# Layers 2 and 3 of a graph network: row buffers for slots, products over their input, expert sums on GpSimd, a last layernorm in two operations

## The chip, the core and the metric

The kernel runs on one core of one Trainium2 chip. The metric is the device time of one execution in microseconds: the time before is the median of five runs. The engines go by the profile's names: PE is TensorE (PEld its weight loads), DVE VectorE, ACT ScalarE, POOL GpSimd, SP SyncE, which here only issues DMAs (its queue is SPq). All data are 32-bit floats.

## The reference

`x` has 1875 nodes of 256 values. Four layers follow, each a graph block and a feed-forward block, both added to `x` after a layernorm. The change is in the last two layers:

```python
# layer 2, graph: two normalized graph convolutions
h = relu(gcn_conv(layernorm(x), edges, weight, W1, b1)); h = gcn_conv(h, edges, weight, W2, b2)
x = x + softmax(h)
# layer 2, feed-forward: 8 experts, the best two by softmax(xt @ Wr + br); xt = layernorm(x)
xn = layernorm(xt) * ln_g[e] + ln_b[e]
x = x + sum over the two experts e of weight_e * (gelu(xn @ W1[e] + b1[e]) @ W2[e] + b2[e])
# layer 3, graph; xl = layernorm(x)
x = x + xl + relu(gcn_conv(xl, edges, weight, W, b))
# layer 3, feed-forward: 16 experts, the best two by xt @ gate_w + gate_b; xt = layernorm(x)
y = xt + sum over the two experts e of weight_e * (relu(xt @ w1[e] + b1[e]) @ w2[e] + b2[e])
x = x + layernorm(y) * gamma + beta
```

`gcn_conv` scales by the inverse root of the degrees on both sides of an adjacency matrix with edge weights.

## The kernel before

The 1875 nodes are padded to 15 tiles of 128 (`NT` = 15, the last one with 83 true rows), and `self.x` holds them all on the chip as `[128, 15, 256]`. The weighted adjacency matrix was built in layer 0 as 15 dense column tiles in DRAM. The code is written for a framework that puts every instruction on its engine in an order that it plans itself, and inserts the waits; tiles come from pools, and the room of a closed pool is given to the next one, which waits for what used it. A tile in a pool with `bufs=n` has n buffers in turn.

**A graph convolution** is `fast_gcn`. Its first loop turns each tile on PE (`turned`, L495, copied from PSUM by ACT as `xT`, L496), multiplies with the weight (`ph`, L1017) and scales into `h` (L1019). Its second loop makes each output tile as 15 products `adj[t][:, u] x h[:, u]` in PSUM (`acc`, L1023), adds (`o`, L1026), scales and adds the bias (`v`, L1028), and calls `done`. In layer 2 it runs twice, as `d0` and `d1`, both with an `h` of their own; in layer 3 once, as `d2`, with `h` written over the input (`inplace`). The adjacency tiles are loaded by `adjacency_tiles` (L995).

**Routing** runs behind the last convolution of a layer: `route_behind` calls `route2` or `route3` for groups of tiles `RG` (four of 3 tiles, one of 2, one of 1), one group after the tile that follows it, the last two after the last tile. A route makes a layernorm (`rxl` in layer 2, `f3y` in layer 3), the router's logits, the two best experts, and a slot for each (node, expert) by counts over the nodes before. Then it fills `rows`, `[128, g, 2, 258]`: the 256 values twice, a gate (L1753) and the token's number (L1754), and sends them to DRAM by indirect DMAs from POOL, one for each tile and choice, six for a group of three (`scatter`, L1122). `rows` lies in a pool with one buffer. In layer 2 the fill is a second layernorm on DVE (L1194) and a copy on ACT (L1929), in layer 3 two copies on ACT (L1961).

**The experts** (`few_experts`) take tiles of 256 slots, load each tile's expert weights, and scatter weighted outputs to `r.outs`. After the last scatter has landed (`done`, L1139) the two rows of each node are summed: for each of 15 tiles one DMA on SP loads both into `s` (L1892, six buffers), and DVE adds the one and then the other into `acc` (L1894), which is `self.x` in layer 2 and `r.y` (`f3y`) in layer 3.

**The end** (`layer3_ffn`): in chunks of 3 tiles the layernorm of `f3y` into `z` (L1194), times gamma (L1205), plus beta (L1206), plus `self.x` (L1977), and a store (L1979, and L1981 for the last 83 rows).

`layernorm` makes statistics for each tile (L1187, L1188), then a chain of small operations for the inverse root (L1190, a Sqrt on ACT at L1167, L1174 to L1179), then one operation for each tile. In the graph blocks of layers 2 and 3 it goes in groups of 5 tiles; in layer 3 POOL then adds it to `x` in three operations (L1073).

Of the kernel before, what the change touches and what calls it, by code (L numbers as in the profile page):

```python
# [31 lines left out]
F32 = mybir.dt.float32  # L32
I32 = mybir.dt.int32
BF16 = mybir.dt.bfloat16
AF = mybir.ActivationFunctionType
# [5 lines left out]
P = 128  # L41
# [33 lines left out]

SL = 256
SH = SL // P

RG = [range(0, 3), range(3, 6), range(6, 9), range(9, 12), range(12, 14), range(14, 15)]

# [17 lines left out]
class Net:  # L98
# [900 lines left out]
    def gcn_weights(self, sb, i, w, b):  # L999
        return self.weight(sb, w, f"gw{i}"), self.vector_row(sb, b, f"gb{i}")  # L1000

    def fast_gcn(self, pre, x, adj, wb, done, inplace=False):


        nc, tc = self.nc, self.tc
        with ExitStack() as ctx:
            one = ctx.enter_context(tc.tile_pool(name=f"{pre}6", bufs=1))
            sb = ctx.enter_context(tc.tile_pool(name=f"{pre}7", bufs=2))
            ps = ctx.enter_context(tc.tile_pool(name=f"{pre}9", bufs=2, space=PSUM))
            w, b = wb  # L1010
            h = x if inplace else one.tile([P, NT, D], F32, name="h")
            for t in range(NT):
                xT = sb.tile([P, KD, P], F32, name="xT")
                self.turned(xT, x[:, t, :], ps)
                p = ps.tile([P, D], F32, name="ph")
                for kc in range(KD):
                    nc.tensor.matmul(p, xT[:, kc, :], w[:, kc, :], start=kc == 0,  # L1017
                                     stop=kc == KD - 1)
                nc.vector.tensor_scalar(h[:, t, :], p, self.dinv[:, t:t + 1], None, op0=ALU.mult)  # L1019
            for t in range(NT):  # L1020
                acc = ps.tile([P, D], F32, name="acc")
                for u in range(NT):
                    nc.tensor.matmul(acc, adj[t][:, u, :], h[:, u, :], start=u == 0,  # L1023
                                     stop=u == NT - 1)
                o = sb.tile([P, D], F32, name="o")
                nc.vector.tensor_tensor(o, h[:, t, :], acc, ALU.add)  # L1026
                v = sb.tile([P, D], F32, name="v")
                nc.vector.scalar_tensor_tensor(v, o, self.dinv[:, t:t + 1], b,  # L1028
                                               op0=ALU.mult, op1=ALU.add)
                done(t, v, sb, ps)  # L1030

    def fast_layer2_gnn(self, r):
        nc, tc, a = self.nc, self.tc, self.a
        with tc.tile_pool(name="q2a", bufs=1) as ap, tc.tile_pool(
            name="q2", bufs=1
        ) as one, tc.tile_pool(name="q2r", bufs=1) as rp:
            ws = [self.gcn_weights(one, i, a[f"L2_gnn_W{i}"], a[f"L2_gnn_b{i}"]) for i in (1, 2)]
            adj = self.adjacency_tiles(ap)
            y = one.tile([P, NT, D], F32, name="y")
            with tc.tile_pool(name="q2n", bufs=3) as sb:  # L1040
                self.layernorm_by(y, self.x, sb, 5)

            def relu(t, v, sb, ps):
                nc.scalar.activation(y[:, t, :], v, AF.Relu)

            def softmax(t, v, sb, ps):
                mx = sb.tile([P, 1], F32, name="mx")
                nc.vector.tensor_reduce(mx, v, AX.X, ALU.max)
                nc.vector.tensor_scalar(mx, mx, -1.0, None, op0=ALU.mult)
                e = sb.tile([P, D], F32, name="e")  # L1050
                sm = sb.tile([P, 1], F32, name="sm")
                nc.scalar.activation(e, v, AF.Exp, bias=mx, accum_out=sm)
                nc.vector.reciprocal(sm, sm)
                nc.vector.scalar_tensor_tensor(self.x[:, t, :], e, sm, self.x[:, t, :],
                                               op0=ALU.mult, op1=ALU.add)
                self.route_behind(self.route2, r, t, rp, ps)

            self.fast_gcn("d0", y, adj, ws[0], relu)
            self.fast_gcn("d1", y, adj, ws[1], softmax)

    def fast_layer3_gnn(self, r):
        nc, tc, a = self.nc, self.tc, self.a
        with tc.tile_pool(name="q3a", bufs=1) as ap, tc.tile_pool(
            name="q3", bufs=1
        ) as one, tc.tile_pool(name="q3r", bufs=1) as rp:
            ws = self.gcn_weights(one, 3, a["L3_gnn_W"], a["L3_gnn_b"])
            adj = self.adjacency_tiles(ap)
            xl = one.tile([P, NT, D], F32, name="xl")
            with tc.tile_pool(name="q3n", bufs=3) as sb:
                self.layernorm_by(xl, self.x, sb, 5)  # L1070
                for t in range(0, NT, 5):
                    v = self.x[:, t:t + 5, :]
                    nc.gpsimd.tensor_tensor(v, v, xl[:, t:t + 5, :], ALU.add)  # L1073
# [7 lines left out]
            self.fast_gcn("d2", xl, adj, ws, add, True)  # L1081

# [98 lines left out]
    def layernorm(self, out, x, sb):  # L1181
# [11 lines left out]
        for t in range(n):  # L1193
            nc.vector.tensor_scalar(out[:, t, :], x[:, t, :], mv[:, t, 0:1], rs[:, t:t + 1],  # L1194
                                    op0=ALU.subtract, op1=ALU.mult)

    def layernorm_by(self, out, x, sb, n):

# [474 lines left out]
    def router(self, name, en, w, b, sb):  # L1673
# [24 lines left out]
                       allow_small_or_imprecise_dtypes=True)  # L1698
        return r

    def route(self, r, ts, x, fill, weigh, sb, ps):


# [29 lines left out]
        at = sb.tile(shape, F32, name="at")  # L1733
        nc.vector.tensor_tensor(at, r.seen[:, sl, :], counts[1], ALU.add)
        nc.vector.tensor_tensor(at, at, r.base[:, None, :].to_broadcast(shape), ALU.add)
        rows = sb.tile([P, g, 2, D + 2], F32, name="rows")
        fill(rows)
        for i in range(2):
            pick = sb.tile(shape, F32, name="pick")
# [74 lines left out]
    def few_experts(self, pre, r, act, f, acc, w1n, w2n, b2n, affine):  # L1814
# [7 lines left out]
        with ExitStack() as ctx:  # L1822
# [64 lines left out]
            with tc.tile_pool(name=f"{pre}s", bufs=2) as sb:  # L1887
                for t in range(NT):
                    n = min(P, N - t * P)
                    s = sb.tile([P, 2, D], F32, name="sum", bufs=6)  # L1890
                    v = r.outs[0:2 * NP, :].rearrange("(i n) d -> n i d", i=2)
                    self.behind(nc.sync.dma_start(s[:n], v[t * P:t * P + n]), done)  # L1892
                    for i in range(2):
                        nc.vector.tensor_tensor(acc[:n, t, :], acc[:n, t, :], s[:n, i, :], ALU.add)  # L1894

    def prepare_experts(self, sb):

# [12 lines left out]
    def route2(self, r, ts, sb, ps):  # L1910
        nc = self.nc
        g = len(ts)
        xl = sb.tile([P, g, D], F32, name="rxl")
        self.layernorm(xl, self.x[:, ts[0]:ts[0] + g, :], sb)

        def weigh(lo, sb):
            pr = sb.tile([P, g, R], F32, name="pr")
# [7 lines left out]
            return hots, tops  # L1925

        def fill(rows):
            self.layernorm(rows[:, :, 0, 0:D], xl, sb)
            nc.scalar.copy(rows[:, :, 1, 0:D], rows[:, :, 0, 0:D])  # L1929

        self.route(r, ts, xl, fill, weigh, sb, ps)

# [56 lines left out]
    def route_all(self, route, r):  # L1989
        with self.tc.tile_pool(name="ra", bufs=2) as sb, self.tc.tile_pool(  # L1990
            name="rap", bufs=2, space=PSUM
        ) as ps:
            for ts in RG:
                route(r, ts, sb, ps)

# [248 lines left out]
```

## Time and profile before

| | |
|---|---|
| median of 5 runs | 3758.53 us (3757.52 to 3762.1) |
| the profiled execution's own time | 3758.14 us |
| its span, first to last instruction | 3756.3 us |
| mean granted TensorE clock | 0.887 |
| busy: PE, DVE, ACT, POOL | 2896.1, 1892.9, 924.6, 1548.5 us |
| products of `d0`, solid on PE | 2600.3 to 2695.6 us |
| products of `d1` with routing between them | 2717.0 to 2844.6 |
| rest of layer 2's routing | 2844.6 to 2882.0 |
| layer 2's experts | 2882.0 to 3229.0 |
| sums, layernorm of layer 3 | 3229.0 to 3268.4 |
| first loop of `d2` | 3268.4 to 3290.8 |
| products of `d2` with routing | 3290.8 to 3408.9 |
| rest of layer 3's routing | 3408.9 to 3437.5 |
| layer 3's experts | 3437.5 to 3700.3 |
| sums | 3700.3 to 3723.6 |
| last layernorm and stores | 3723.6 to 3756.3 |

The lower rows were read from the order of time. Busy time is time in which the engine worked on an instruction, and its idle time matters only where the next step waits for it. A line such as "DVE rows L1754 <- DMA f_slots<-rows,slot" means that VectorE was idle before its instruction of line 1754, which writes `rows`, and that the last thing to release it was a DMA that reads `rows` and writes `f_slots`. An "x3" counts instructions that were merged into a line of the timeline.

### The profile page before, as it was taken

To read this page: it belongs to the slowest core of one execution; us is meant where nothing else is said; L and a number is where in the kernel's file an instruction comes from. 1 tells how busy PE (TensorE), PEld (TensorE's weight loads), DVE (VectorE), ACT (ScalarE), POOL (GpSimd) and SP (SyncE) were. 2 spreads that over 40 slices of the span, in tenths; PEclk is the share of its full clock that TensorE was granted. 3 is DMA by queue.
4 is the path that set the end of the run, shared out by engine and by line. 5 is a ranking of instruction groups with operands and counts; after the bars stand their busy time and mean duration, and the time that the engine had idled before them with its cause. 6 is when DMAs were issued, how large, how long until landed. Compare 5 with 4: busy or idle time off the path is not lost. (4 is left out here: it accounts for less than half of the span.)

```text
span 3756.3 us, 43452 instructions
## 1 busy us (share of the span) xinstructions
PE 2896.1 (77%) x14049; PEld 2405.9 (64%) x14049; DVE 1892.9 (50%) x5542; ACT 924.6 (25%) x1998; POOL 1548.5 (41%) x1546
## 2 busy tenths in 40 slices
PE   3878789979997999668745654985995999596993
PEld 2667678858876777446534444654874888475772
DVE  5566576756765776683256663015254111444234
ACT  1333233323332333213211110210132222122221
POOL 2777577747775777100277861001011111112220
PEclk9999899989998999889866765997997999798996
DMA  5434656655664543113444431524003555503663
GB/s 147 124 109 129 200 158 201 181 152 162 186 194 129 141 115 114 41 38 96 150 130 132 138 102 38 163 79 170 1 22 97 188 182 183 212 31 110 205 202 120
DMA packets 330704, 495.34 MB, mean 132 GB/s; under 512 B 79601, under 2 KB 258724, under 8 KB 328676
## 3 DMA queue, kind: packets, MB, share of 16 engines
q1 hardware_dynamic: 254612, 289.88, 24.5%
q0 software_dynamic: 72672, 199.68, 18.0%
q10 hardware_dynamic: 3184, 2.91, 0.2%
q8 instruction: 113, 1.85, 0.2%
q14 instruction: 123, 1.01, 0.1%
HBM read 369.90 MB, written 122.43 MB: 131 GB/s over the span
## 5 line engine op out<-in xcount | busy, mean ns | idle before, releaser
L1116 POOL DMA_INDIRECT g<-qt,w_src x1056 | 1033.7, 979 | 431.3 <-issue 350.5
L621 PE MATMUL acc<-m,s 128*128 128x256 f32 (+1 forms) x2112 | 559.9, 389 | 16.3 <-ACT m L608 16.3
L592 PE MATMUL pe<-ew,w_attr 128*128 128x256 f32 x1888 | 509.4, 395 | 72.3 <-DVE g L607 71.5
L607 DVE TENSOR_TENSOR g<-g,pe 128x512 f32<-128x512 f32 x528 | 360.5, 683 | 394.0 <-DMA g<-qt,w_src 327.2
L608 ACT ACTIVATE m<-g 128x512 f32<-128x512 f32 x528 | 332.6, 631 | 791.1 <-DVE g L607 604.5
L1116 POOL DMA_INDIRECT g<-rq_h,w_tsrc x264 | 305.5, 1157 | 391.1 <-PE pz L886 311.2
L592 PEld LDWEIGHTS pe<-ew,w_attr 128*128 128x128 f32 x1888 | 364.8, 197 | 155.5 <-DVE g L607 95.5
L621 PEld LDWEIGHTS acc<-m,s 128*128 128x128 f32 x2112 | 404.5, 196 | 65.3 <-ACT m L608 17.5
L1874 PE MATMUL hid<-xeT,w 128*128 128x256 f32 x1184 | 272.9, 387 | 23.5 <-DVE xeT L1869 23.5
L1880 PE MATMUL out<-w,hidT 128*128 128x256 f32 x1184 | 264.0, 379 | 0.0
L1874 PEld LDWEIGHTS hid<-xeT,w 128*128 128x128 f32 x1184 | 222.1, 193 | 62.8 <-DVE xeT L1869 30.8
L1876 ACT ACTIVATE hidT<-hid,cols 128x256 f32<-128x256 f32 x296 | 138.2, 474 | 447.3 <-PE hid L1874 447.3
L1880 PEld LDWEIGHTS out<-w,hidT 128*128 128x128 f32 x1184 | 225.1, 190 | 30.5
L1122 POOL DMA_INDIRECT f_slots<-rows,slot x60 | 58.3, 972 | 416.2 <-DVE pick L1740 248.6
L599 DVE TENSOR_TENSOR s<-iota,w_dst 128x256 f32<-128x256 f32 x528 | 219.8, 417 | 0.0
L399 PE MATMUL padj<-col,row 128*128 128x240 f32 x720 | 206.5, 382 | 14.5 <-DVE col L372 13.0
L1023 PE MATMUL acc<-h,adj 128*128 128x256 f32 x900 | 207.4, 389 | 0.0
L1883 DVE TENSOR_TENSOR ye<-out,b 128x256 f32<-128x256 f32 x104 | 44.1, 424 | 313.9 <-PE out L1880 313.9
L1023 PEld LDWEIGHTS acc<-h,adj 128*128 128x128 f32 x900 | 172.7, 195 | 22.4
L1122 POOL DMA_INDIRECT f_outs<-ye,f2place x44 | 42.7, 970 | 302.4 <-DVE ye L1884 276.5
L399 PEld LDWEIGHTS padj<-col,row 128*128 128x128 f32 x720 | 142.1, 199 | 36.3 <-DVE col L372 9.9
L372 DVE TENSOR_SCALAR col<-wide,g_col,g_wt 128x240 f32<-128x240 f32 x360 | 147.3, 409 | 0.0
(416 smaller groups left out, 4070.6 us busy)
## 6 DMA issues: line engine op xcount, KB each, us to landing
f_slots<-zeros SPq DMA_DIRECT2D x45, 1032.0 KB
w<-in_L_ffn_W SPq DMA_DIRECT2D x44, 1024.0 KB
adj<-adj SPq DMA_DIRECT2D x45, 960.0 KB
w<-in_L_ffn_w SPq DMA_DIRECT2D x60, 512.0 KB
w<-in_L_ffn_w SPq DMA_DIRECT2D x18, 1024.0 KB
g<-qt,w_src POOLq DMA_INDIRECT x1056
dstrow<-lin SPq DMA_DIRECT2D x14, 1152.0 KB
rq_h<-hr SPq DMA_DIRECT2D x8, 1980.0 KB
```

The source lines that it names most:

```text
L372: pin(nc.vector.tensor_scalar(col, self.wide, self.gcol[:, i:i + 1], self.gwt[:, i:i + 1], op0=ALU.is_equal, op1=ALU.mult))
L399: pin(nc.tensor.matmul(pa[:, u // GT, :], row, col, start=u % GT == 0, stop=u % GT == GT - 1))
L592: pin(nc.tensor.matmul(pes[q][:, v, :], at[:, v, :], self.ew[:, i, :], start=True, stop=True))
L599: pin(nc.vector.tensor_tensor(ss[q], self.iota[:, None, :].to_broadcast([P, 2, P]), self.wdst[:, c:c + 2, None].to_broadcast([P, 2, P]), A ...
L607: pin(nc.vector.tensor_tensor(g, g, pes.pop(q), ALU.add))
L608: pin(nc.scalar.activation(m[:, :, :D], g, AF.Relu))
L621: pin(nc.tensor.matmul(accs[t], s[:, v, :], m[:, v, :], start=k == v == 0, stop=end and v == 1))
L1023: nc.tensor.matmul(acc, adj[t][:, u, :], h[:, u, :], start=u == 0, stop=u == NT - 1)
L1116: self.nc.gpsimd.indirect_dma_start(out=out, out_offset=None, in_=table, in_offset=bass.IndirectOffsetOnAxis(ap=at, axis=0))
L1874: nc.tensor.matmul(p1, w1[:, kc, m * P:(m + 1) * P], xT[:, kc, :], start=kc == 0, stop=kc == KD - 1)
L1876: nc.scalar.activation(hT[:, m, :], p1, act, bias=v[:, m:m + 1])
L1880: nc.tensor.matmul(p2, hT[:, m, i * P:(i + 1) * P], w2[:, m, :], start=m == 0, stop=m == fc - 1)
```

## The change

`rows` is no longer a tile of its own: `rows_in` cuts two buffers out of a given tile, and each route takes the other one. In layer 2 that tile is `first`, which holds the first convolution's input and, as both convolutions now write over their input, its products; in layer 3 it is a tile `rowbufs`. The layernorms of the graph blocks go in groups of 3, and layer 3's sum with `x` is made on POOL tile by tile. `layernorm` is cut in two, `moments` and the scaling. The fill of layer 2 becomes six ACT operations with a scale and a bias. The sums of the expert outputs have 15 buffers, loads on two queues (SP and ACT), the sum of the two rows on POOL and one add on DVE. At the end beta is added to `x` ahead of the experts on POOL, and the last layernorm is two operations for each tile, in place, without `z`.

```diff
+ROWS = 2 * CH * 2 * (D + 2)
...
-    def fast_gcn(self, pre, x, adj, wb, done, inplace=False):
+    def fast_gcn(self, pre, x, adj, wb, done):
...
-            one = ctx.enter_context(tc.tile_pool(name=f"{pre}6", bufs=1))
...
-            h = x if inplace else one.tile([P, NT, D], F32, name="h")
+            h = x
...
+            first = one.tile([P, NT, D], F32, name="first")
             y = one.tile([P, NT, D], F32, name="y")
+            self.rows_in(r, first)
             with tc.tile_pool(name="q2n", bufs=3) as sb:
-                self.layernorm_by(y, self.x, sb, 5)
+                self.layernorm_by(first, self.x, sb, CH)
...
-            self.fast_gcn("d0", y, adj, ws[0], relu)
+            self.fast_gcn("d0", first, adj, ws[0], relu)
...
+            self.rows_in(r, one.tile([P, 1, ROWS], F32, name="rowbufs"))
             with tc.tile_pool(name="q3n", bufs=3) as sb:
-                self.layernorm_by(xl, self.x, sb, 5)
-                for t in range(0, NT, 5):
-                    v = self.x[:, t:t + 5, :]
-                    nc.gpsimd.tensor_tensor(v, v, xl[:, t:t + 5, :], ALU.add)
+                for t in range(0, NT, CH):
+                    self.layernorm(xl[:, t:t + CH, :], self.x[:, t:t + CH, :], sb)
+                    for u in range(t, t + CH):
+                        nc.gpsimd.tensor_tensor(self.x[:, u, :], self.x[:, u, :], xl[:, u, :],
+                                                ALU.add)
...
+    def rows_in(self, r, buf):
+        flat = buf.rearrange("p t d -> p (t d)")
+        n = ROWS // 2
+        r.rows = [flat[:, i * n:(i + 1) * n].rearrange("p (g i d) -> p g i d", i=2, d=D + 2)
+                  for i in range(2)]
...
-        rows = sb.tile([P, g, 2, D + 2], F32, name="rows")
+        r.rows.append(r.rows.pop(0))
+        rows = r.rows[0][:, :g]
         fill(rows)
...
-                    s = sb.tile([P, 2, D], F32, name="sum", bufs=6)
+                    s = sb.tile([P, 2, D], F32, name="sum", bufs=NT)
                     v = r.outs[0:2 * NP, :].rearrange("(i n) d -> n i d", i=2)
-                    self.behind(nc.sync.dma_start(s[:n], v[t * P:t * P + n]), done)
-                    for i in range(2):
-                        nc.vector.tensor_tensor(acc[:n, t, :], acc[:n, t, :], s[:n, i, :], ALU.add)
+                    queue = nc.scalar if t % 2 else nc.sync
+                    self.behind(queue.dma_start(s[:n], v[t * P:t * P + n]), done)
+                    nc.gpsimd.tensor_tensor(s[:n, 0, :], s[:n, 0, :], s[:n, 1, :], ALU.add)
+                    nc.vector.tensor_tensor(acc[:n, t, :], acc[:n, t, :], s[:n, 0, :], ALU.add)
...
         def fill(rows):
-            self.layernorm(rows[:, :, 0, 0:D], xl, sb)
-            nc.scalar.copy(rows[:, :, 1, 0:D], rows[:, :, 0, 0:D])
+            mv, rs = self.moments(xl, sb)
+            low = sb.tile([P, g], F32, name="rlow")
+            nc.vector.scalar_tensor_tensor(low, mv[:, :, 0], -1.0, rs, op0=ALU.mult, op1=ALU.mult)
+            for i in range(2):
+                for j in range(g):
+                    nc.scalar.activation(rows[:, j, i, 0:D], xl[:, j, :], AF.Identity,
+                                         bias=low[:, j:j + 1], scale=rs[:, j:j + 1])
...
-        self.few_experts("e3", r, AF.Relu, 2 * D, y, "L3_ffn_w1", "L3_ffn_w2", "L3_ffn_b2", False)
         with tc.tile_pool(name="f3b", bufs=1) as one, tc.tile_pool(name="f3s", bufs=3) as sb:
-            z = one.tile([P, NT, D], F32, name="z")
             gam = self.vector_row(one, a["L3_ffn_gamma"], "gam")
             bet = self.vector_row(one, a["L3_ffn_beta"], "bet")
+            for t in range(NT):
+                nc.gpsimd.tensor_tensor(self.x[:, t, :], self.x[:, t, :], bet, ALU.add)
+            self.few_experts("e3", r, AF.Relu, 2 * D, y, "L3_ffn_w1", "L3_ffn_w2", "L3_ffn_b2",
+                             False)
             for t in range(0, NT, CH):
-                v, ts = z[:, t:t + CH, :], slice(t, t + CH)
-                self.layernorm(v, y[:, ts, :], sb)
-                self.affine(v, gam, bet)
-                nc.vector.tensor_tensor(v, v, self.x[:, ts, :], ALU.add)
+                ts = slice(t, t + CH)
+                v = y[:, ts, :]
+                mv, rs = self.moments(v, sb)
+                for j in range(CH):
+                    u = v[:, j, :]
+                    nc.vector.scalar_tensor_tensor(u, u, mv[:, j, 0:1], gam, op0=ALU.subtract,
+                                                   op1=ALU.mult)
+                    nc.vector.scalar_tensor_tensor(u, u, rs[:, j:j + 1], self.x[:, t + j, :],
+                                                   op0=ALU.mult, op1=ALU.add)
```

More of the change, by code (lines that the diff above doesn't have):

```diff
@@ L1079, in add @@
                 self.route_behind(self.route3, r, t, rp, ps)
-            self.fast_gcn("d2", xl, adj, ws, add, True)
+            self.fast_gcn("d2", xl, adj, ws, add)
     def first_edges(self):
@@ L1179, in inverse, with moments @@
         nc.vector.tensor_tensor(out, r, q, ALU.mult)
-    def layernorm(self, out, x, sb):
+    def moments(self, x, sb):
         nc = self.nc
@@ L1192, in layernorm @@
         self.rsqrt(rs, ve, sb)
-        for t in range(n):
-            nc.vector.tensor_scalar(out[:, t, :], x[:, t, :], mv[:, t, 0:1], rs[:, t:t + 1],
-                                    op0=ALU.subtract, op1=ALU.mult)
+        return mv, rs
+    def layernorm(self, out, x, sb):
+        mv, rs = self.moments(x, sb)
+        for t in range(x.shape[1]):
+            self.nc.vector.tensor_scalar(out[:, t, :], x[:, t, :], mv[:, t, 0:1], rs[:, t:t + 1],
+                                         op0=ALU.subtract, op1=ALU.mult)
     def layernorm_by(self, out, x, sb, n):
@@ L1913, in route2 @@
         xl = sb.tile([P, g, D], F32, name="rxl")
-        self.layernorm(xl, self.x[:, ts[0]:ts[0] + g, :], sb)
+        mv, rs = self.moments(self.x[:, ts[0]:ts[0] + g, :], sb)
+        for j in range(g):
+            nc.vector.tensor_scalar(xl[:, j, :], self.x[:, ts[0] + j, :], mv[:, j, 0:1],
+                                    rs[:, j:j + 1], op0=ALU.subtract, op1=ALU.mult)
         def weigh(lo, sb):
@@ L1927, in fill @@
         def fill(rows):
-            self.layernorm(rows[:, :, 0, 0:D], xl, sb)
-            nc.scalar.copy(rows[:, :, 1, 0:D], rows[:, :, 0, 0:D])
+            mv, rs = self.moments(xl, sb)
+            low = sb.tile([P, g], F32, name="rlow")
+            nc.vector.scalar_tensor_tensor(low, mv[:, :, 0], -1.0, rs, op0=ALU.mult, op1=ALU.mult)
+            for i in range(2):
+                for j in range(g):
+                    nc.scalar.activation(rows[:, j, i, 0:D], xl[:, j, :], AF.Identity,
+                                         bias=low[:, j:j + 1], scale=rs[:, j:j + 1])
         self.route(r, ts, xl, fill, weigh, sb, ps)
@@ L1992, in route_all @@
         ) as ps:
+            self.rows_in(r, sb.tile([P, 1, ROWS], F32, name="rowbufs", bufs=1))
             for ts in RG:
```

## The prediction

> **What bounds the kernel now.** I read the chain that ended last, then a table of stretches that I cut at the borders of layers 2 and 3, then the waits inside them, then the order of time around each. The change touches nothing before 2564 us. First the stretches (busy us per engine, granted clock, DMA share, GB/s):
>
> ```profile
> core 0: us, PE busy (x) PEld busy (x) DVE busy (x) ACT busy (x) POOL busy (x), PEclk, DMA share, GB/s
> 2717.00:2844.60 127.60, 114.41 (x524) 99.57 (x522) 72.58 (x365) 41.02 (x76) 20.72 (x21) 0.91 0.06 22
> 2844.60:2882.00 37.40, 6.85 (x26) 5.61 (x26) 21.86 (x149) 9.74 (x17) 8.79 (x11) 0.56 0.32 98
> 3229.00:3268.40 39.40, 1.09 (x4) 0.70 (x4) 28.02 (x94) 0.66 (x4) 6.72 (x8) 0.50 0.69 252
> 3290.80:3408.90 118.10, 109.13 (x525) 93.53 (x524) 56.61 (x249) 27.87 (x51) 20.86 (x22) 0.97 0.07 24
> 3700.30:3723.60 23.30, 0.00 (x0) 0.00 (x0) 12.71 (x44) 1.49 (x2) 0.00 (x0) 0.50 0.54 166
> 3723.60:3748.40 24.80, 0.00 (x0) 0.00 (x0) 24.56 (x79) 0.82 (x4) 0.00 (x0) 0.50 0.19 64
> ```
>
> Rows 1 and 4 are the adjacency products with routing between them: PE sets the pace but loses 13 and 9 us. Row 2 is the routing tail, where PE has nothing. Rows 3 and 5 sum the expert outputs; the last row is the final layernorm, with DVE full. Now the waits in the routing of layer 2 (first three lines) and of layer 3:
>
> ```profile
> engine line waited for: us in total, times, longest us
> PE mm L495 <- DVE rxl L1194: 23.1, 4, 10.0
> DVE rows L1754 <- DMA f_slots<-rows,slot: 20.3, 4, 7.2
> ...
> DVE rows L1754 <- DMA f_slots<-rows,slot: 33.5, 4, 8.6
> ACT rows L1961 <- DMA f_slots<-rows,slot: 15.4, 2, 10.3
> ```
>
> DVE stands at the write of token numbers into `rows` until the six scatters of the route before have read it, and PE stands behind DVE. In order of time (start, duration):
>
> ```profile
> 2280.13 0.17 DVE L1754 TENSOR_SCALAR rows<-token 128x3 f32<-128x3 f32 x2
> ...
> 3257.01 2.88 POOL L1073 TENSOR_TENSOR x<-x,xl 128x1280 f32<-128x1280 f32 x1 [26.94 <-DVE xl L1194]
> 3257.32 2.60 DVE L1176 TENSOR_TENSOR rs_q<-rs_r 128x5 f32<-128x5 f32 x1
> ...
> 3268.37 0.65 ACT L496 COPY xT<-mm 128x256 f32<-128x256 f32 x2 [5.39 <-DVE xl L1194]
> ...
> 3333.58 0.24 DVE L1754 TENSOR_SCALAR rows<-token 128x3 f32<-128x3 f32 x2 [8.34 <-DMA f_slots<-rows,slot]
> ...
> 3722.51 1.09 DVE L1894 TENSOR_TENSOR f3y<-f3y,sum 83x256 f32<-83x256 f32 x3 [6.09 <-DMA sum<-f_outs]
> ```
>
> The first line decides most of what follows: the token write of layer 2's first route ran 470 us before that route, in layer 1. So the compiled order is not the program's: an instruction goes to where the plan thinks its buffer is free.
>
> **The change, part by part.** The profiled execution took 3758.14 us, span 3756.3, so 1.8 lie around it; the median is 3758.53. I sum against 3758.14; the 0.4 is noise.
>
> *Two row buffers.* The obvious gain is the DVE waits (20.3 and 33.5 us) and PE's behind them. I do not count it. With one buffer the token write of route k+1 was put where the plan thought the scatters of route k done, and DVE stood there. With two, the writes of routes 1 and 2 find free buffers, but that of route 3 becomes free at the same event, the end of route 1's scatters, depends on nothing else, and will fill the same gap on DVE. The one wait shifts by one route and stays; behind it DVE holds the next `o` (L1026), hence the next layernorm and PE's transposes, as now. What must go is only the wait after route 5, for then no route is left. In layer 2 that is the fill's 2.62 us at 2872.6 (L1194). In layer 3 it is ACT's fill, waiting from 3427 to 3432.2, which holds the last scatters back by about 2.4, and ACT's fill at 3415.9, which holds two transposes' copies back, some 1.5. Layer 2: -2.6 (0 to -10). Layer 3: -4, before what POOL adds below.
>
> *Fill of layer 2's rows.* Three DVE writes of 0.33 in place of each route leave, one small one of 0.17 comes, and on ACT six 128x256 operations of 0.42 (the Relu row) replace one copy of 0.83: 1.7 us more per route, in the order in which the scatters, 1.27 apart, want them. Taken as nothing: the plan can put them behind DVE's slot arithmetic, which takes 3 us from the fill to the first scatter. If that cover is gone it costs 1.7 per route, 3 in the tail. No row shows an Identity; Copy and Relu ran between Sqrt and Exp without a table load, so 0 is nearer than a load's 1.28 per route. The Trainium skill, "ScalarE: Activation LUTs", section "Table sets: the hidden batching unit", has cheap functions such as identity in every set, which no run here shows; by it the load is none.
>
> *Products over their input (layer 2).* Before, `h` (15 KB) took the room that the layernorm's small tiles left, and `xT` came behind. In layer 3, which already works in place, `xT` lies in that room itself: ACT waited with it until the last layernorm write (3268.37 above) though PE had transposed by 3256.8. From there to the solid products took 22.4 us (3290.8); in layer 2 it took 20.0 from the first `h` at 2580.3. So layer 2 gets layer 3's start: +2.4. Groups of 3 for 5 add two chains of seven small operations, some 0.55 each: +1.1. Sum +3.5 (0 to +5.5).
>
> *Sums of expert outputs (layer 2 to 3).* The issues took 12.2 us for 15, because six buffers had to come free; with 15 buffers on two queues they take about 4 (8 of 0.49). But the last transfer, 83 rows, ran alone at 24 GB/s for 7.5 us where the full tiles together reached 365, so it looks like one engine of 16. That engine also carries a sixteenth of 3.6 MB, 224 KB, and 166 KB of its own: 390 KB at 23.5 GB/s is 16.6 us from 3231, 3248 to 3250 against 3251.3. DVE keeps 15 adds of 0.42 out of 30. POOL gets 15 sums, and 15 adds of 128x256 for 3 of 128x1280. Their price: 2.88 us for 1280 is 0.58 for 256 by proportion; with a fixed part like that of small POOL operations (0.1) I take 0.65; upper bound 1.2, if the fixed part is a quarter of the 2.88. The rows at 3257 show what else it costs: a DVE add of 0.16 took 2.60, until POOL was done. This happened twice, 4.8 us; bn_stats beside POOL was not stretched. Shorter POOL operations let DVE through more often, but there are 30. Of the 17 us from 3251.3 to 3268.4 I take off 1.5 for the earlier landing and 3.5 for layernorm done during the wait and shorter blocks: -5 (-11 to +3).
>
> The rule that speaks against this is in the Trainium skill, "SBUF — State Buffer", section "Who interferes with whom": a DVE instruction with two SBUF inputs and a GpSimd one that reads SBUF exclude each other for a whole instruction. The trace agrees (2.60 for 0.16).
>
> *Bias on POOL (layer 3).* gam and bet now load into room that the adjacency tiles leave, so not before 3408.9, when the first weights went out too. 14 of the 15 adds are then ready at once, 9 us of POOL between the last scatter of route 4 (3411.7) and the first of route 5 (3425.9). They fit, but block DVE's small adds in the tail's arithmetic: +2.5 (0 to +8). With the -4: -1.5.
>
> *Final sums and layernorm.* Landing as above: 3719.5, POOL 0.65, DVE at 3721.2 for 3722.5: -1.3. Per chunk, scale 0.96, two products and an add of 0.85 each make 3.5; six two-step operations at 0.45 make 2.7: -0.8, five times -4. Ten of the 15 statistics (0.41) lay behind the last sum; with DVE half free some 8 can come before: -3.2. Sum -8.5 (-4 to -14). The last store, 7.9 us, stays.
>
> Sum: +3.5 -2.6 -5 -1.5 -8.5 = -14.1, so **3744 us**; its own range 3728 to 3758.
>
> **Rivals.** *The second buffer does end the stalls.* For: it is what 54 us of waits ask for, and if the plan puts the token write behind the fill, nothing blocks. Against: 2280.13. In layer 2 first scatters are 31.8, 28.0 and 29.2 us apart, in layer 3 26.1, 27.1, 26.8; three tiles of 6.47 and 3.4 of routing on PE make 22.8. Gain 20.6 and 11.5, and 5 in each tail: 3744 - 42 = 3702.
>
> *POOL becomes the bound (slower).* One mechanism: a 128x256 POOL add costs 1.2 and shuts DVE out. Then 30 adds at the border last 36 us from 3232.7 (start of layer 3's products not before 3269, with DVE's chains held +5), 14 bias adds push route 5's scatters by about +10, the end gains only 2. +3.5 -2.6 +5 +10 -2 = +14: 3772. It decides from about 1.0 us per add. For: exclusion is measured. Against: 2.25 ns per column.
>
> *Gains cancel:* the last 83 rows land no earlier and layernorm stays behind them, so -4 at the end and 0 at the border: 3758.1 - 4 - 4.1 (both tails) + 3.5, 3754.
>
> **How the numbers follow.** Forecast 0.56, stalls ended 0.24, POOL bound 0.11, cancelled 0.09. A measurement of this kernel tells about 0.2%, 7.5 us. Of the forecast's range about a sixth lies within that; so faster 0.56 x 0.83 + 0.24 = 0.71, same 0.18, slower 0.11. The range takes in most of the first two cases and the third's near edge: 3697 to 3761.
>
> **What would show it.** Right: L1754 still waits 4 times per layer for `f_slots`, now for the route before the last; first scatters 26 to 30 us apart; ACT's first `xT` of layer 2 waits for the last layernorm write; the 83-row sum lands 18 us after the first issue; POOL adds of 0.6 to 0.7; 2.7 us per chunk at the end. Wrong: no wait at L1754 and scatters 23 apart (the first rival), or POOL adds over 1 us with DVE adds stretched to their length (the second).

## The result, and the profile after

The median after is 3750.9 us (30 runs, 3741.8 to 3760.0) against 3758.7 before (50 runs, 3752.6 to 3768.0): a ratio of 0.9977, 95% interval 0.9972 to 0.9982. The change makes the kernel faster by 0.23%, about 8 us. The profiled execution took 3747.6 us, span 3745.7, so it lies 10.5 below that of before and 3.3 below its own median.

The line numbers of after: token write L1773, gates L1772, scatter L1128, layernorm scaling L1205 (in a route of layer 2 L1936), first copies L498, sum with `x` on POOL L1078, bias on POOL L2000, sums of the expert outputs L1913 (POOL) and L1914 (DVE), last layernorm L2009 and L2011.

The stretches of after, in the view that the prediction opened with (the columns are those of its first row), in the same order:

```profile
core 0: us, PE busy (x) PEld busy (x) DVE busy (x) ACT busy (x) POOL busy (x), PEclk, DMA share, GB/s
2717.00:2848.00 131.00, 115.67 (x517) 100.89 (x516) 68.50 (x354) 49.71 (x94) 18.24 (x19) 0.88 0.05 19
2848.00:2885.80 37.80, 9.90 (x41) 7.96 (x39) 22.06 (x148) 13.50 (x23) 11.24 (x12) 0.57 0.35 109
3230.70:3269.90 39.20, 1.09 (x4) 0.70 (x4) 29.62 (x91) 2.35 (x7) 23.03 (x34) 0.50 0.74 273
3291.97:3408.90 116.93, 108.46 (x527) 92.23 (x525) 56.87 (x250) 29.31 (x54) 21.98 (x23) 0.99 0.07 26
3696.90:3718.20 21.30, 0.00 (x0) 0.00 (x0) 11.94 (x21) 1.28 (x1) 12.29 (x16) 0.50 0.58 181
3718.20:3737.80 19.60, 0.00 (x0) 0.00 (x0) 19.33 (x86) 1.02 (x5) 0.00 (x0) 0.50 0.24 82
```

The rounds of layer 2 (first row) got longer, at a lower clock. The border (third row) kept its length although POOL now does 23 us of work in it. The last row, DVE's layernorm, is 5.2 us shorter. The waits of the routing in layer 2 (first two lines) and layer 3 (engine, line, what it waited for: sum in us, times, longest):

```profile
DVE first L1773 <- DMA f_slots<-first,slot: 27.5, 8, 6.4
PE mm L497 <- DVE rxl L1936: 24.4, 4, 9.1
...
DVE rowbufs L1773 <- DMA f_slots<-rowbufs,slot: 28.3, 8, 4.5
PE mm L497 <- DVE f3y L1205: 16.5, 4, 9.8
```

The token write still waits for the scatters, after as before, in spite of two buffers. What the instruction line says of its first four instances, and then DVE's order of time around the first scatters (2753.2 us):

```profile
L1773 DVE TENSOR_SCALAR first<-token x4: 168/168/169, 2692.5 to 2695.5; 128x3 f32<-128x3 f32 x4
```

```profile
2755.23 0.18 DVE L1195 BATCH_NORM_AGGREGATE ln_mv<-ln_st 128x2 f32<-128x6 f32 x1
2758.68 0.17 DVE L1773 TENSOR_SCALAR first<-token 128x3 f32<-128x3 f32 x1 [3.27 <-DMA f_slots<-first,slot]
2758.76 0.41 DVE L1028 TENSOR_TENSOR o<-y,acc 128x256 f32<-128x256 f32 x1
2759.21 0.49 DVE L1030 SCALAR_TENSOR_TENSOR v<-o,dinv,gb 128x256 f32<-128x256 f32 x1
2762.38 0.17 DVE L1773 TENSOR_SCALAR first<-token 128x3 f32<-128x3 f32 x1 [2.69 <-DMA f_slots<-first,slot]
2762.46 0.41 DVE L1052 TENSOR_REDUCE mx<-v 128x1 f32<-128x256 f32 x1
```

Four token writes, those of routes 1 and 2, run at 2692 to 2696 us, before any routing. The two at 2758.68 and 2762.38 are those of route 3, and stand behind route 1's scatters. Before, both halves (i = 0 and 1) stood in one place behind the tile's `mx` (one line of x2), so ACT's exponential ran during the wait:

```profile
2756.65 0.15 DVE L1049 TENSOR_SCALAR mx<-mx 128x1 f32<-128x1 f32 x1
2761.41 0.24 DVE L1754 TENSOR_SCALAR rows<-token 128x3 f32<-128x3 f32 x2 [4.60 <-DMA f_slots<-rows,slot]
```

Now they are apart and the tile's `o`, `v` and `mx` lie between and behind them.

The other lines that answer to those of the prediction: the first copy of layer 2, POOL beside the layernorm of layer 3 with a DVE operation of 0.15 stretched to 0.68, the bias adds, and the last tile's sum.

```profile
2580.45 0.65 ACT L498 COPY xT<-mm 128x256 f32<-128x256 f32 x2 [2.94 <-DVE first L1205]
...
3257.03 0.68 DVE L1185 TENSOR_TENSOR ln_rs<-rs_r,rs_q 128x3 f32<-128x3 f32 x1
3257.62 0.15 DVE L1182 TENSOR_TENSOR rs_q<-rs_r 128x3 f32<-128x3 f32 x1
...
3265.59 2.23 POOL L1078 TENSOR_TENSOR x<-x,xl 128x256 f32<-128x256 f32 x3 [1.58 <-DVE xl L1205]
...
3413.13 10.30 POOL L2000 TENSOR_TENSOR x<-x,bet 128x256 f32<-128x256 f32 x15 [2.81 <-DMA w<-in_L_ffn_w]
...
3717.07 0.72 POOL L1913 TENSOR_TENSOR sum<-sum 83x256 f32<-83x256 f32 x1 [4.27 <-DMA sum<-f_outs]
3717.82 0.42 DVE L1914 TENSOR_TENSOR f3y<-f3y,sum 83x256 f32<-83x256 f32 x1 [4.40 <-POOL sum L1913]
```

From layer 1's last gather (2556.65 us before, 2556.64 after) to the end the time went as follows. The stages were read from POOL's order of time: the first scatter of each group, and the instant `done` when the last scatter of a stage had landed.

| stage | before | after | difference | forecast |
|---|---|---|---|---|
| gather to first scatter of layer 2 (its start) | 195.42 | 196.58 | +1.2 | +3.5 |
| three rounds of layer 2 (first to fourth group) | 89.02 | 94.32 | +5.3 | 0 |
| its tail, fourth group to done | 40.85 | 38.30 | -2.6 | -2.6 |
| layer 2's experts | 347.04 | 344.81 | -2.2 | 0 |
| done to first scatter of layer 3 (border) | 95.50 | 95.05 | -0.4 | -5 |
| three rounds of layer 3 | 79.98 | 77.34 | -2.6 | 0 |
| its tail | 32.97 | 32.74 | -0.2 | -1.5 |
| layer 3's experts | 262.74 | 261.13 | -1.6 | 0 |
| done to the end | 56.13 | 48.79 | -7.3 | -8.5 |
| sum | 1199.65 | 1189.06 | -10.6 | -14.1 |

The experts' code is the same in both. In the runs below they took 345.4 to 347.1 us in layer 2 and 261.2 to 262.8 in layer 3 (264.0 in e6, which moves work into them), so most of -2.2 and -1.6 is variation from run to run. Without these two rows the stages that the change touches gave -6.8 of the -10.6.

### The profile page after: what moved, and what is told of

Read it like the earlier page. It is cut to its first block, busy times and chain, and to the rows that moved or that the text cites. A ratio compares the mean times of both kernels' runs of the same rounds, so it can differ in the third digit from the quotient of the medians.

```text
span 3745.7 us, 43548 instructions
## 1 busy us (share of the span) xinstructions
PE 2894.0 (77%) x14049; PEld 2402.5 (64%) x14049; DVE 1893.8 (51%) x5527; ACT 935.9 (25%) x2026; POOL 1584.0 (42%) x1603
## 3 DMA queue, kind: packets, MB, share of 16 engines
q0 software_dynamic: 72672, 199.68, 18.1%
## 5 line engine op out<-in xcount | busy, mean ns | idle before, releaser
L1893 PE MATMUL hid<-xeT,w 128*128 128x256 f32 x1184 | 271.4, 386 | 23.5 <-DVE xeT L1888 23.5
L1899 PE MATMUL out<-w,hidT 128*128 128x256 f32 x1184 | 264.0, 379 | 0.0
L401 PE MATMUL padj<-col,row 128*128 128x240 f32 x720 | 207.6, 383 | 15.1 <-DVE col L374 14.1
L1128 POOL DMA_INDIRECT f_outs<-ye,f2place x44 | 42.7, 970 | 300.5 <-DVE ye L1903 276.3
L1128 POOL DMA_INDIRECT f_slots<-first,slot x30 | 29.5, 983 | 284.1 <-issue 229.6
L983 PE MATMUL acc<-g,s 128*128 128x264 f32 x528 | 140.6, 425 | 5.5 <-issue 3.0
L1128 POOL DMA_INDIRECT f_outs<-ye,f3place x60 | 57.5, 959 | 201.6 <-DVE ye L1903 198.8
```

What stands on the lines that cost most here:

```text
L401: pin(nc.tensor.matmul(pa[:, u // GT, :], row, col, start=u % GT == 0, stop=u % GT == GT - 1))
L983: nc.tensor.matmul(acc, s[:, j, :], g[:, j, :], start=j == 0, stop=j == n - 1)
L1128: return self.nc.gpsimd.indirect_dma_start(out=table, out_offset=bass.IndirectOffsetOnAxis(ap=at, axis=0), in_=in_, in_offset=None, **kw)
L1893: nc.tensor.matmul(p1, w1[:, kc, m * P:(m + 1) * P], xT[:, kc, :], start=kc == 0, stop=kc == KD - 1)
L1899: nc.tensor.matmul(p2, hT[:, m, i * P:(i + 1) * P], w2[:, m, :], start=m == 0, stop=m == fc - 1)
```

## The experiments

Each is compared by this same time from the last gather to the end, in its profiled execution, and by the ratio of its time to that of the kernel before. Experiments e5 to e8 ran on another chip, on which the work up to that gather took longer (2977 to 2991 us, 2561 in e1) and the kernel before 4194.0 us; behind the gather their unchanged stages are as in the others (layer 2's rounds to 0.03 us). A difference of one or two microseconds between two profiled executions can be variation: stages of the same code differ by as much. The kernel before, run beside each, took 3761.2 us with e1 to e4 and 3758.0 with e9 to e12.

| kernel | last gather to end | time, us | ratio to before (95%) |
|---|---|---|---|
| before | 1199.65 | 3758.7 | |
| after | 1189.06 | 3750.9 | 0.9977 (0.9972 to 0.9982) |
| e1, token and gate tied to the slots | 1149.03 | 3706.9 | 0.9856 (0.9839 to 0.9872) |
| e2, the same in before | 1161.83 | 3720.0 | 0.9894 (0.9878 to 0.9909) |
| e3, after with DVE adds | 1192.44 | 3752.2 | 0.9981 (0.9971 to 0.9991) |
| e4, after with 80 + 3 rows | 1187.60 | 3746.4 | 0.9966 (0.9954 to 0.9978) |
| e5, e1 + open pool | 1136.69 | 4118.1 | 0.9819 (0.9786 to 0.9851) |
| e6, e1 + bias later | 1146.67 | 4140.0 | 0.9873 (0.9837 to 0.9908) |
| e7, e1 + x on ACT | 1147.20 | 4142.7 | 0.9871 (0.9833 to 0.9908) |
| e8, e1 + all of 83 rows split | 1141.31 | 4133.0 | 0.9839 (0.9798 to 0.9880) |
| e9, e1 with one buffer | 1154.06 | 3711.8 | 0.9879 (0.9864 to 0.9894) |
| e10, e1 with the fill on DVE | 1148.43 | 3707.2 | 0.9864 (0.9849 to 0.9880) |
| e11, the gains together | 1117.18 | 3674.7 | 0.9781 (0.9768 to 0.9795) |
| e12, e11 + x on ACT | 1110.82 | 3669.4 | 0.9767 (0.9753 to 0.9780) |

**e1 and e2: is it the order or the buffers?** `s` is the slot, a number that only the route itself can give; `r.token` holds token numbers for both choices.

```diff
-            nc.vector.tensor_copy(rows[:, :, i, D:D + 1], gates[i][:, :, None])
-            nc.vector.tensor_scalar(rows[:, :, i, D + 1:], self.token[:, sl, None], float(i * NP),
-                                    None, op0=ALU.add)
+            for c, v in ((D, gates[i]), (D + 1, r.token[:, i, sl])):
+                nc.vector.scalar_tensor_tensor(rows[:, :, i, c], s, 0.0, v, op0=ALU.mult,
+                                               op1=ALU.add)
```

> Kernel after, but the gate and the token number are written as (slot x 0 + gate) and (slot x 0 + token), so that neither can be placed ahead of its own route's slots. Theory of the prediction (the stall at the token write is an accident of the compiled order, not a lack of buffers): no wait for f_slots on DVE in either layer, first scatters of layer 2 23 to 27 us apart instead of 32.2, 31.5, 30.6, of layer 3 22.5 to 25 instead of 25.9, 27.0, 24.4; time 15 to 35 below the kernel after, 3716 to 3736. Rival (the stall only fills time in which the rounds wait for something else, such as DVE's small operations): gaps within 1 us of those of after, time within 4 us of it.

> Kernel before, with its one buffer, and gate and token number tied to the slots in the same way. Theory of the prediction: the order was the fault, so one buffer is enough inside the rounds (the fill comes some 20 us after the scatters of the route before began): gaps as in e1 within 1.5 us, only the tail keeps its waits (the fill's 2.6 us in layer 2, ACT's in layer 3); time 15 to 32 below the kernel before. Rival (two buffers are what is needed): the wait moves to the fill, L1194 and L1961, with 4 waits of 3 us or more in each layer, and the time is within 5 us of before.

e1: the waits for `f_slots` at the token write are gone, the groups of layer 2 come 22.7, 22.9 and 23.0 us apart, of layer 3 23.5, 21.9 and 22.2, at the low end of what was expected or below it, and the time falls by 40.0 us in the profile against after (44 in the medians), more than the 35 that the expectation allowed. The rounds of layer 2 in e1's table of stretches:

```profile
2721.00:2828.00 107.00, 104.85 (x526) 90.92 (x525) 69.64 (x356) 49.38 (x94) 18.98 (x19) 1.00 0.07 23
```

PE is busy for 104.85 of 107 us at the full clock: now it is the bound. e2, with one buffer and all else as before, has the same rounds (22.9, 22.8, 22.8 and 23.2, 22.2, 22.2) and is 37.8 below before, again more than expected (32). Of its waits in layer 2 (first line) and layer 3 those of the fill remain, all but one of 2.3 us in the tails, and one of 1.6 us at the tied write:

```profile
DVE rows L1194 <- DMA f_slots<-rows,slot: 5.2, 2, 2.6
...
ACT rows L1965 <- DMA f_slots<-rows,slot: 19.3, 3, 11.7
```

So the stall came from the place of one small instruction in DVE's order, and a second buffer alone did not remove it. (Both runs tie the write of the gate too, at which DVE waited once before, for 1.8 us.)

**e9 and e10: what the second buffer and the fill on ACT are worth.** In e9 both buffers are cut from the same room; in e10 the fill is that of before.

```diff
# e9
-        r.rows = [flat[:, i * n:(i + 1) * n].rearrange("p (g i d) -> p g i d", i=2, d=D + 2)
+        r.rows = [flat[:, :n].rearrange("p (g i d) -> p g i d", i=2, d=D + 2)
# e10
+            self.layernorm(rows[:, :, 0, 0:D], xl, sb)
+            nc.scalar.copy(rows[:, :, 1, 0:D], rows[:, :, 0, 0:D])
```

> Kernel e1, but both row buffers are the same room, so that a route must wait for the scatters of the one before. Everything else of the change and the tied writes stay. Theory (inside the rounds the scatters are long done when the next fill comes; two buffers are worth something in the tails alone, where routes follow each other closely): gaps of the first three rounds 22.5 to 23.2 in layer 2 and 21.9 to 23.6 in layer 3 as in e1, tails 3 to 5 us longer than 32.1 and 31.0; from layer 1's last gather to the end 1155 to 1159 us instead of 1149. Rival (two buffers are what freed the rounds): gaps over 25, 1165 or more.

> Kernel e1, but layer 2's rows are filled as before, by a layernorm on DVE and one copy on ACT. Theory of the prediction (the move to ACT is neutral, as the six ACT operations lie beside DVE's slot arithmetic): layer 2's gaps 22.5 to 23.2, its tail within 1 us of 32.1, 1148 to 1150.5 from the last gather to the end. Rival (DVE is what the rounds or the tail wait for, so the fill costs there): tail 33.5 or more, 1151 to 1156.

e9 costs 5.0 us, a little under what was expected, 4.0 of them in the two tails, and the rounds are e1's to a hundredth or two. The tail of layer 3 is longer by 3.7 (34.67 against 30.99); that of layer 2 is not (32.42 against 32.07), which the expectation had wrong. e10 is equal to e1 (tail 32.30). e2, which has one buffer and the fill on DVE, took 36.14; it differs from e1 in the rest of the change too. So far as it can be compared, this says: in layer 2's tail either the second buffer or the fill on ACT is enough, and both together bring no more than one.

**e3 and e4: the sums.**

```diff
# e3
-                    nc.gpsimd.tensor_tensor(s[:n, 0, :], s[:n, 0, :], s[:n, 1, :], ALU.add)
-                    nc.vector.tensor_tensor(acc[:n, t, :], acc[:n, t, :], s[:n, 0, :], ALU.add)
+                    for i in range(2):
+                        nc.vector.tensor_tensor(acc[:n, t, :], acc[:n, t, :], s[:n, i, :], ALU.add)
# e4
+                    m = n - n % 16
+                    for lo, hi in ((0, m), (m, n)):
+                        if lo < hi:
+                            self.behind(queue.dma_start(s[lo:hi], v[t * P + lo:t * P + hi]), done)
```

> Kernel after, but both rows of each node are added by DVE as before (30 DVE adds, no POOL sums). Theory A (the landing of the last 83 rows sets the border, and the POOL sums cost DVE about what they take off it): from the last scatter's done to layer 3's first xT 38 to 40 us against 39.2, end stage 48 to 50 against 48.8; time within 3 us of after. Theory B (the POOL sums cost: they shut DVE out while layernorm and statistics are due): border 34 to 36, end stage 46 to 47; time 5 to 7 below after.

> Kernel after, but the last tile's load of 83 rows is two loads, 80 rows and 3 rows. Theory A (83 rows go through one DMA engine of 16, 166 KB at 23 GB/s, and this sets both borders): the last landing comes 5 to 7 us earlier after done (now 20.2 and 20.9 us), no stretch at 23 GB/s is left, time 6 to 12 below after. Theory B (the last load is late because it shares the engines with all others): landing within 1 us of after, time within 3.

e3 measured 40.15 us from done to the first copy and 48.92 at the end, against 39.20 and 48.79: POOL's sums bring 1 us at the border and nothing at the end. That is theory A, with the border 0.15 above its range. In e4 the last stretch of the loads is gone. GB/s in slices of 0.625 us from about the last done, after first, then e4:

```profile
GB/s 0 21 133 197 251 369 385 384 360 354 349 346 347 354 343 344 357 347 344 274 61 23 23 25 23 23 25 23 23 25 23 5 0 0 13 0 0 13 0 0
```

```profile
GB/s 0 8 200 292 380 362 349 300 365 372 374 361 344 347 346 354 344 354 351 292 64 0 0 13 0 0 0 13 0 0 0 0 0 0 0 0 92 352 185 0
```

In after the 83 rows still run at 23 GB/s, alone for 6 us; with 80 and 3 rows nothing is left of that, and the loads end some 6.5 us earlier, as theory A said. The Trainium skill, "DMA: Bandwidth & Descriptors", section "Why a DMA increments its semaphore by 16 and not by 1", says that the number of engines is the largest one up to 16 that divides the slowest dimension on both sides of the transfer, hence one engine for a prime number of rows above 16. e4 agrees. The time did not follow: 6 to 12 us were expected, the medians differ by 4.5 and the intervals of the two ratios overlap. What was gained on the way is smaller than the earlier landing: the last DVE add comes 3.8 us earlier after done at the end (17.12 for 20.91) and 1.8 at the border (19.24 for 21.00). POOL is next:

```profile
3241.04 12.63 POOL L1916 TENSOR_TENSOR sum<-sum 128x256 f32<-128x256 f32 x15 [4.51 <-DMA sum<-f_outs]
```

Fifteen adds without a gap, 0.84 each, until 18.2 us after done. The end is 5.0 shorter and the way to layer 3's first scatter 2.2; start, rounds and tail of layer 2, where e4 is the same kernel as after, took 4.0 us more in this run and the experts there 1.2, so the whole of the profile shows 1.5. No run has the split loads with DVE's own adds, so what POOL's sums cost once the landing is out of the way stays open.

**e5 to e8, four parts on top of e1.** Open pool: the graph convolution's lines are indented into the `with` of the layernorm's pool, so that its room is not given to `xT`; in layer 3 the Relu also writes over its input. The others:

```diff
# e6: the 15 bias adds wait for the last routing scatter
+                    self.behind(nc.gpsimd.tensor_tensor(self.x[:, t, :], self.x[:, t, :], bet,
+                                                        ALU.add), filled)
# e7: up = 1 + rs, low = -mean * rs; replaces POOL's add
+                        nc.scalar.activation(self.x[:, t + u, :], self.x[:, t + u, :], AF.Identity,
+                                             bias=low[:, u:u + 1], scale=up[:, u:u + 1])
# e8: e4's loads, and the last store
+                    nc.sync.dma_start(self.out[full * P:full * P + m, :], v[:m, full - t, :])
+                    nc.scalar.dma_start(self.out[full * P + m:, :], v[m:n, full - t, :])
```

> Kernel e1, but the pool of the layernorm's small tiles stays open during the graph convolutions of layers 2 and 3, so that the copies of transposed tiles lie elsewhere (in layer 3 the Relu writes over its input to make room). Theory of the prediction (the first copies wait for the layernorm's last write because they lie in its room): the first copy of layer 2 comes 8 us earlier, the first o 2 to 3 us earlier after layer 1's last gather (47.7 to 48.2 instead of 50.2), in layer 3 from done to the first scatter 92 to 93 instead of 94.8; time 4 to 5 below e1. Rival (the layernorm itself sets the start, the copies are free work ahead of it): both starts within 0.7 us of e1's, time within 1.5.

> Kernel e1, but the 15 bias adds on POOL wait until the last scatter of layer 3's routing has landed, so that they run beside the first loads of the experts. Theory of the prediction (they block DVE's small operations in the routing tail): tail from the fourth group's first scatter to done 28 to 29 us instead of 31.0, experts unchanged at 262, time 2 to 3 below e1. Rival (the tail is set by PE, ACT and the scatters, and the stretched small operations have room): tail 30.5 to 31.5, time within 1 of e1.

> Kernel e1, but layer 3's x + xl is made by ACT, as x times (1 + rs) minus mean times rs, in 15 operations of some 0.5 us, and not by POOL. Theory A (POOL's 15 adds of 0.74 shut out DVE's small two-input operations and stretch the scalings from 1.03 to 1.45): done to layer 3's first xT 33 to 35 us instead of 38.9, time 4 to 6 below e1. Theory B (the chains of small operations after the last landing set this time by their own length): 37.5 to 40, time within 1.5 of e1.

> Kernel e1, with both loads of 83 rows split into 80 and 3 rows as in e4, and the last store of 83 rows into 80 on SP and 3 on ACT. Theory A (a transfer of 83 rows runs on one engine; 83 KB at 23 GB/s are 3.6 us): border 2 us shorter and the end stage's DVE work 4.5 earlier as in e4, and the last store 3 us shorter, from 7.7 to 4.5 to 5 after its issue; time 8 to 11 below e1. Theory B (the store's time is a fixed cost of a DMA): the store takes 7 to 8 as before; time 5 to 7 below e1.

| from | e1 | e5 | e6 | e7 | e8 |
|---|---|---|---|---|---|
| last gather to first `xT` of layer 2 | 23.81 | 14.36 | 23.81 | 23.81 | 23.81 |
| last gather to first `o` | 50.16 | 42.12 | 50.33 | 50.31 | 50.27 |
| done to first `xT` of layer 3 | 38.91 | 26.30 | 38.87 | 36.52 | 36.70 |
| done to first scatter of layer 3 | 94.82 | 88.35 | 94.83 | 92.11 | 92.11 |
| tail of layer 3 | 30.99 | 31.58 | 26.25 | 31.35 | 32.26 |
| layer 3's experts | 262.21 | 262.41 | 264.00 | 261.98 | 261.48 |
| done to DVE's last operation | 40.62 | 41.04 | 40.83 | 40.77 | 36.31 |
| from there to the end | 7.95 | 8.00 | 8.06 | 8.00 | 6.42 |

e5: the theory, and three times its size: 8.0 us in layer 2 and 6.5 in layer 3, not 2.4 each. e6: the tail is 4.7 shorter, twice the 2.5 that the prediction charged, but 1.8 come back in the experts, where the adds now stand beside the first tile's work. e7: 2.4 to the first copy, between the two theories. e8: border and end as expected; the store gained 1.5, not 3, so its theory A holds for half, and the whole gained 7.7 for the 8 to 11 expected. The data of the store have moved 4 us before the span ends in e8, and no view says what the rest of the time is.

**e11 and e12: together.** e5 and e8 in one, with the bias adds spread one by one behind the scatters of the experts' tiles 4 to 18; e12 adds e7.

> Kernel e1 with the pool of the layernorm's small tiles left open (e5), both loads and the last store of 83 rows split (e8), and the 15 bias adds on POOL one by one behind the scatters of the experts' tiles 4 to 18. Sum of the parts: open pool -12.3, splits -7.7, bias -4 (tail 26 to 27 as in e6, experts back at 262): 1125 us from the last gather to the end instead of 1149. If the open pool's and the splits' gains at the border overlap (both shorten the way to layer 3's products), 1127 to 1129.

> Kernel e11, but layer 3's x + xl on ACT as in e7. If POOL's adds still stretch DVE's layernorm, 2 us less than e11, 1123. If ACT, which now also copies the first transposed tiles during the layernorm, becomes what layer 3's start waits for: 0 to 4 us more than e11.

e11 took 1117.2 us, 8 less than the plain sum of the parts: done to the first scatter of layer 3 is 84.4, 10.5 below e1, and the tail 24.2 with the experts at 261.9. e12 brought 6.4 more in the profile (5.3 in the medians), for the 2 expected, 5.0 of them at the border (79.4), where e7 alone had brought 2.7: with the pool open PE and ACT no longer wait for the whole layernorm, so each chunk that comes earlier can count; this is argued from the code and not tested by itself. e12 is 2.3% below before (0.9767).

## Why the prediction was right and where it was not

The forecast was -14.1 us, the medians give -7.8: inside its range, and a little over half of its size. The profile without the experts gives -6.8. Of what is missing the border has 4.5 us, the rounds 2.7, layer 3's tail 1.3 and the end 1.2; the start came out 2.3 better than forecast.

**Right: the stall stays.** "The one wait shifts by one route and stays" is what the trace shows, for the reason given, a write that depends on nothing of its route. The first rival, "the second buffer does end the stalls", was priced at 42 us; e1, which does what that rival made its condition (the token write behind the route's own work), measured 40.0. Its price was right and its condition not met: against the kernel before, e1's rounds are 20.4 and 12.4 us shorter, for the 20.6 and 11.5 of the prediction. The fill's term of 0 held as well: the six Identity operations of a route run behind the Sqrt in 3.06 us with no table load among them, and e10 is equal to e1.

**Mis-sized: the rounds, 0 in the sum, +5.3 in layer 2 and -2.6 in layer 3.** "Stays" was taken as "stays as long". The wait of both halves in one place became two waits with a tile's `o`, `v` and `mx` between and behind them. It happened 8 times per layer and not the 4 forecast, 27.5 us for 20.3 in layer 2 and 28.3 for 33.5 in layer 3. Within the three rounds alone the waits sum to 19.1 us for 13.1 and to 23.2 for 25.2, that is +6.1 and -2.0, close to what the rounds changed. First scatters came 32.2, 31.5 and 30.6 us apart in layer 2 and 25.9, 27.0 and 24.4 in layer 3, for the 26 to 30 forecast. That the waits set the rounds is shown by e1. That the split made them longer in layer 2 is read from the order of time; no run put the halves together again, and in layer 3 the waits became shorter with the same split, so the split alone does not explain both.

**Right in kind: layer 2's start, +3.5, measured +1.2.** The first copy did wait for the layernorm's last write (2580.45). The first `o` came 1.4 later than before in this run, 2.5 to 2.8 in e1, e3 and e4. The size was off because layer 2's start before, against which layer 3's was measured, was held too: the first `h` came at 2580.28, right behind the layernorm's last write (2578.46 to 2580.16). So the 2.4 is only the difference of two late starts. With the room kept open, e5 gave 6.5 us in layer 3 and put layer 2's start 5.6 ahead of before's.

**Right: the tails' buffers.** -2.6 in layer 2 as said, though e9 and e10 show that the fill on ACT would have done it too. In layer 3 e9 gives 3.7 for the -4. The other half of that term, +2.5 for the bias adds, was too small: 4.7 by e6. These two, measured on top of e1, would make +1.0; the tail measured -0.2 for the -1.5.

**Wrong step: the border, -5, measured -0.4.** Of the two amounts in it the earlier landing came (20.2 us after done for 22.4; DVE's add of the last tile 1.4 earlier, 1.5 was counted). "3.5 for layernorm done during the wait and shorter blocks" did not: from that add to the last scaling DVE took 18.1 us for 16.6 before, which used up the 1.4. Layernorm did not move into the wait: 3 of the 15 statistics ran ahead of the last tile's sum, for 5 before. The blocks did not get shorter in sum. POOL's smaller adds stretched DVE in more places: four operations of some 0.15 took 0.65 to 0.68, two more 0.43 and 0.48, and the three scalings of a chunk 1.43 to 1.78 in all five chunks, against 1.02 to 1.06 at layer 2's start. That is about 5.0 us in all, for the 4.7 of the two blocks before. e7 takes these adds away and gains 2.7, e3 takes the others away and gains nothing. The rule cited against the change ("SBUF — State Buffer", "Who interferes with whom", in the Trainium skill) was the better guide here than the shorter blocks. At the border the outcome of the third rival came, about 0, though the rows did land earlier; its total of 3754 lies nearer to the measured 3750.9 than the forecast's 3744.

**Near: the end, -8.5, measured -7.3.** The last add came 1.4 earlier (1.3 was said). From it to DVE's last operation 25.9 became 19.9, -6.0 for -7.2: statistics did not move into the wait. Twelve of 15 lay behind the last sum, for 10 before. DVE's adds beside POOL took mostly 0.7 to 0.9 and filled a part of the wait, but not all: DVE stood idle for 4.40 us right ahead of the last sum (3.62 at the border), with statistics of tiles long summed behind it in its order. That is the same pattern as at the token write; why the plan put them there no run shows.

**The second rival,** POOL as the bound from about 1.0 us per add, did not come: adds took 0.72 alone and 0.84 each in a row beside DVE's, for the 0.65 forecast. e4 shows how near it was: with the landing out of the way POOL's 15 adds in a row set the end of the border's sums.

## What to carry to other kernels

Before adding a buffer for a wait, look at where the waiting instruction stands: a write that depends on little is placed as soon as the plan thinks its room free, and in an engine that works in order all behind it waits too. Giving it an operand that only its own step can produce brought 40 us here, where the second buffer brought 5 at most. Look the same way at what a first tile's room held before, and at transfers with a prime number of rows.

## What the runs showed of the hardware

A stall cost more than its own length, since PE's clock fell with it: the rounds of layer 2 have 524 matmuls in 114.4 us of busy PE at a clock of 0.91 before, 517 in 115.7 at 0.88 after, and 526 in 104.9 at 1.00 in e1. In after PE is busy for 2.40 us from 2793 to 2799, behind a wait of DVE for the scatters, and from 2799 to 2809 the granted clock is 0.50, with 29 matmuls in 8.13 us. The Trainium skill, "TensorE: Matmul & The Clock Gate", section "HAM oscillation — how this bites in real kernels", describes waits between groups of matmuls that return PE to half its clock each time, and these rows agree. A row count of 83 made both a load (166 KB) and a store (83 KB) run at 23 GB/s; 80 and 3 rows did not. By a line through two sizes, POOL's adds cost 2.1 ns per column and 0.18 us besides (2.88 us for 1280 columns, 0.72 for 256).
